# Two softmax attentions in steps of four heads, and a routed layer that gathers its tokens by indirect transfers

## The chip, the cores and the metric

The kernel runs on one core of a Trainium2 chip as one program. The metric is the time of one execution on the device in microseconds. Two runs of the kernel before took 3570.28 and 3580.17 us (median 3575.23). The engines are TensorE (PE, with its weight loads as PEld), VectorE (DVE), ScalarE (ACT), GpSimd (POOL) and SyncE (SP), which only issues transfers. ACT and POOL can issue transfers too, from their own queues.

## The reference

Four layers follow one another on x of shape (32, 256, 128): each adds an attention-like block of the normalised x, and then a feed-forward block of the normalised x. Three of these eight blocks matter here.

- The feed-forward block of layer 0. A softmax over 16 experts gives every token 16 scores. In each batch row (256 tokens) every expert takes the 32 tokens that score highest for it, computes `(gelu(x Wg) * (x Wu)) Wd` with 256 hidden channels, weighs the result with the score and adds it back at the token's place. A shared expert of the same form runs over all tokens.
- The attention of layer 2: 16 heads of 8 channels over 256 tokens, causal, with q, k and v through a rank-32 bottleneck: `softmax(q k^T / sqrt(8)) v`, then an output matrix.
- The attention in the feed-forward block of layer 3: again 16 heads of 8 channels over 256 tokens, with biases and without a mask. A routed expert layer follows it.

All of it is in float32; the attentions of the kernel split q and k into a high and a low half for it.

## The kernel before, in words

**Attention** (`attention`, lines 1118 to 1411) serves both softmax attentions. Heads are taken in pairs: one on partitions 0 to 63 (j = 0), the other on partitions 64 to 127 (j = 1). A batch has 8 pairs, and there are 32 batches. Its pieces are:

- `project` (transpose of x), `split` (q for i = 0, k for i = 1; high and low half, through DRAM into the layout by heads) and `load_values`. `split` writes each half twice into a DRAM tile `d` (line 1218), and reads it back with one transfer of 32 partitions for each j (line 1224). For q it also clears two rows (line 1226, `q<-k`).
- `maxima`: scores with queries on the partitions into a tile `s` of two PSUM banks, one for each head, and a single DVE reduction over both (line 1259).
- `lower` and `place`: the negated maxima, split into halves and turned into rows. DVE copies the rows out of PSUM (line 1287), and four transfers on SP put them into the q tile (line 1292, `q<-row`), so that the next scores come out with the maximum already subtracted.
- `weights`: scores with keys on the partitions into two tiles `t`, and two ACT exponentials (line 1314).
- `values`: exponentials times values, four heads together, into `o` (line 1327).
- `collect`, `turn`, `back` and `finish`: division by the sum, output matrix, addition.

For the causal attention, `cover` (line 1182) adds a large negative number to hidden scores by bf16 matmuls, all of one head and then all of the other.

PSUM has 8 banks: two buffers of `s` (pool `ps`, 4 banks), one bank for `o` (`pa`), and a ring of three (`pt`) that `weights` shares with `project`, `split`, `load_values`, `place`, `turn`, `back` and `finish`.

The order on PE, ACT and DVE is the program's (`manual_schedule`). In step t, one pair: `maxima` of the pair 14 steps ahead (`LEAD`), `weights` of pair t, the pieces that are due in that step (table `todo`), and, on every odd step, `values` of the two pairs before. SP and POOL are ordered by the planner of the framework. The q, k and v tiles are rings of four batches (`RING`).

**Layer 0 experts** (`l0_ffn`, lines 425 to 660) have four phases, ordered by the planner: (1) normalise, transpose, router logits, softmax; (2) `choose` (the 32 best of each of 8 rows x 16 experts, four times) and `shared` (16 blocks of 512 tokens); (3) gather: for each batch row a matmul spreads the chosen indices (line 590), DVE compares them with the token numbers (line 597), and two matmuls pick the tokens (line 600); (4) the 16 experts, two halves of 16 batch rows each (lines 624 to 631), and then the scatter by one-hot matmuls for each batch row (lines 643 to 659).

Of the kernel before, what the change touches and what calls it, by code (L numbers as in the profile page):

```python
# [18 lines left out]
P = 128  # L19
# [405 lines left out]
def l0_ffn(K):  # L425
    nc, ins = K.nc, K.ins
    NE, CAP, F = 16, 32, 256
    ES = NE * CAP
    with ExitStack() as es:
        sp = K.pool(es, "f0", 1)  # L430
        xn = sp.tile([P, NT, D], F32, name="xn")


        idx = sp.tile([P, 4, CAP], F32, name="idx")
        tab = sp.tile([P, 4, 2, 8, 4], F32, name="tab")
        gate_w = K.load(sp, "f0_gate_w")
# [4 lines left out]

        same_e = sp.tile([P, NE], F32, name="same_e")
        nc.vector.tensor_reduce(
            same_e, K.ident.rearrange("p (b e) -> p e b", e=NE), axis=AX.X, op=ALU.add
        )
        sel_b = sp.tile([P, 8, P], F32, name="sel_b")
        nc.vector.tensor_copy(
            sel_b,  # L450
            K.block_rows(sp, "blk8", 8).unsqueeze(2).to_broadcast([P, 8, P]),
        )
# [7 lines left out]
        tok = sp.tile([P, 2], F32, name="tok")  # L460
        nc.gpsimd.iota(
            tok, pattern=[[P, 2]], base=0, channel_multiplier=1,
# [8 lines left out]
        with ExitStack() as ts:  # L471
            xp = K.pool(ts, "f0x", 1)
            wk = K.pool(ts, "f0w", 2)
            xnT = xp.tile([P, NBLK, 512], F32, name="xnT")
            sc = xp.tile([P, 2, NB, NE], F32, name="sc")
            with ExitStack() as ps:
                pt = K.pool(ps, "f0pt", 2, PSUM)
                pl = K.pool(ps, "f0pl", 1, PSUM)
                lg = pl.tile([P, 2, NB, NE], F32, name="lg")
                for blk in range(NBLK):  # L480
                    for j in range(4 * blk, 4 * blk + 4):
                        K.normed(xn[:, j, :], j, mean, r)
                    t = pt.tile([P, 512], F32, name="t")
                    K.transpose4(t, xn[:, 4 * blk : 4 * blk + 4, :])
                    nc.scalar.copy(xnT[:, blk, :], t)
                    for i in range(4):
                        nc.tensor.matmul(
                            lg[:, i % 2, 2 * blk + i // 2, :],
                            xnT[:, blk, i * P : (i + 1) * P], gate_w, start=True, stop=True,
                        )  # L490
                K.softmax(
                    xp, sc.rearrange("p h b e -> p (h b) e"), lg.rearrange("p h b e -> p (h b) e")
                )

            pt = K.pool(ts, "f0pt2", 1, PSUM)
            pg = K.pool(ts, "f0pg", 2, PSUM)
            po = K.pool(ts, "f0po", 2, PSUM)

            def choose(q):

                t = pt.tile([P, SEQ], F32, name="st")
                for h in range(2):
                    nc.tensor.transpose(
                        t[:, h * P : (h + 1) * P],
                        sc[:, h, 8 * q : 8 * q + 8, :].rearrange("p b e -> p (b e)"), K.ident,
                    )
                s = wk.tile([P, SEQ], F32, name="s")
                nc.vector.tensor_copy(s, t)
                vi = wk.tile([P, 2, CAP], F32, name="vi")
                iu = wk.tile([P, CAP], mybir.dt.uint32, name="iu")  # L510
                for k in range(CAP // 8):
                    m = vi[:, 1, 8 * k : 8 * k + 8]
                    nc.vector.max(m, s)
                    nc.vector.max_index(iu[:, 8 * k : 8 * k + 8], m, s)
                    if k < CAP // 8 - 1:
                        nxt = wk.tile([P, SEQ], F32, name="s")
                        nc.vector.match_replace(nxt, m, s, -1.0)
                        s = nxt
                nc.vector.tensor_copy(vi[:, 0, :], iu)
                nc.gpsimd.tensor_copy(idx[:, q, :], vi[:, 0, :])  # L520
                vt = pt.tile([64, P], F32, name="vt")
                nc.tensor.transpose(vt, vi.rearrange("p k s -> p (k s)"), K.ident)
                vs = wk.tile([64, P], F32, name="vs")
                nc.vector.tensor_copy(vs, vt)
                o = pt.tile([P, 2, P], F32, name="st")
                for k in range(2):
                    nc.tensor.matmul(
                        o[:, k, :], rep[:, k].rearrange("p a s -> p (a s)"), vs,
                        start=True, stop=True,
                    )  # L530
                own = wk.tile([P, 64, 4], F32, name="own")
                nc.vector.tensor_mul(
                    own, o.rearrange("p k (n a) -> p (k n) a", a=4),
                    own4.unsqueeze(1).to_broadcast([P, 64, 4]),
                )
                nc.vector.tensor_reduce(
                    tab[:, q].rearrange("p k b g -> p (k b g)"), own, axis=AX.X, op=ALU.add
                )

            def shared(blk):  # L540
                h = wk.tile([P, 2, 512], F32, name="h")
                for c in range(2):
                    g = pg.tile([P, 512], F32, name="g")
                    u = pg.tile([P, 512], F32, name="u")
                    cs = slice(c * P, (c + 1) * P)
                    nc.tensor.matmul(g, wsg[:, cs], xnT[:, blk, :], start=True, stop=True)
                    nc.tensor.matmul(u, wsu[:, cs], xnT[:, blk, :], start=True, stop=True)
                    nc.scalar.activation(h[:, c, :], g, AF.Gelu)
                    nc.vector.tensor_mul(h[:, c, :], h[:, c, :], u)
                o = po.tile([P, 4, D], F32, name="o")  # L550
                for i in range(4):
                    for c in range(2):
                        nc.tensor.matmul(
                            o[:, i, :], h[:, c, i * P : (i + 1) * P], wsd[:, c, :],
                            start=c == 0, stop=c == 1,
                        )
                xb = K.x[:, 4 * blk : 4 * blk + 4, :]
                nc.vector.tensor_add(xb, xb, o)

            for q in range(4):  # L560
                choose(q)
                for blk in range(4 * q, 4 * q + 4):
                    shared(blk)


        xs = K.pool(es, "f0s", 1).tile([P, 4, NB, 4, CAP], F32, name="xs")
# [8 lines left out]

        experts = [expert(0), expert(1)]
        with ExitStack() as ps:
            gw = K.pool(ps, "f0g", 2)
            pi = K.pool(ps, "f0pi", 2, PSUM)
            px = K.pool(ps, "f0px", 2, PSUM)  # L580
            for q in range(4):
                bd = gw.tile([P, NE, CAP], F32, name="bd")
                nc.gpsimd.tensor_mul(
                    bd, idx[:, q, :].unsqueeze(1).to_broadcast([P, NE, CAP]),
                    same_e.unsqueeze(2).to_broadcast([P, NE, CAP]),
                )
                for b8 in range(8):
                    b = 8 * q + b8
                    ib = pi.tile([P, ES], F32, name="ib")
                    nc.tensor.matmul(  # L590
                        ib, sel_b[:, b8, :], bd.rearrange("p e s -> p (e s)"),
                        start=True, stop=True,
                    )
                    xg = px.tile([P, ES], F32, name="xg")
                    for h in range(2):
                        pick = gw.tile([P, ES], F32, name=f"pick{h}")
                        nc.vector.tensor_scalar(
                            pick, ib, tok[:, h : h + 1], None, ALU.is_equal
                        )
                        nc.tensor.matmul(  # L600
                            xg, xn[:, 2 * b + h, :], pick, start=h == 0, stop=h == 1
                        )
                    nc.scalar.copy(
                        xs[:, :, b].rearrange("p g a s -> p g (a s)"),
                        xg.rearrange("p (g n) -> p g n", g=4),
                    )


        with ExitStack() as ps:
            hw = K.pool(ps, "f0h", 2)  # L610
            pg = K.pool(ps, "f0eg", 3, PSUM)
            po = K.pool(ps, "f0eo", 2, PSUM)
            for e in range(NE):
# [492 lines left out]
HEADS, HD = 16, 8  # L1106
PAIRS = HEADS // 2
ONE = HD
LEAD = 14
RING = 4  # L1110


# [903 lines left out]
```

## Time and profile before

The profiled execution took 3567.47 us, with a span of 3565.8 us from the first to the last instruction.

| stretch, us from the start | what runs | PE busy | DVE | ACT | POOL | granted clock |
|---|---|---|---|---|---|---|
| 468 to 558 | layer 0: choose and shared | 88.5 | 57.5 | 20.4 | 2.9 | 0.98 |
| 558 to 649 | layer 0: gather by matmul | 88.3 | 45.1 | 18.7 | 2.1 | 1.00 |
| 649 to 822 | layer 0: experts | 173.0 | 65.4 | 38.2 | 0.0 | 1.00 |
| 822 to 903 | layer 0: scatter | 75.3 | 52.6 | 17.2 | 41.9 | 1.00 |
| 1900 to 2200 | layer 2 attention, steady part | 276.5 | 170.8 | 153.2 | 30.6 | 0.98 |
| 2750 to 3050 | layer 3 attention, steady part | 259.2 | 212.5 | 190.2 | 16.7 | 0.99 |

Busy times are in us. A busy PE is not PE at its peak, since the ends of matmuls are modelled. The granted clock is the share of TensorE's full clock that the chip allowed, and it takes the values 0.5 and 1 in stretches of some 3.4 us. The layer 2 attention runs from about 1710 to 2340 us, the one in layer 3 from about 2550 to 3220 us: together more than a third of the span.

### The profile page before, as it was taken

What the parts mean: (1) busy time and instruction counts of PE and PEld (TensorE: products, weight loads), DVE (VectorE), ACT (ScalarE), POOL (GpSimd) and SP (SyncE); (2) the same over time, 40 slices, a digit from 0 to 9 for tenths busy, and PEclk for the clock granted to TensorE, in tenths of its full rate; (3) what the DMA queues carried; (4) which work ended last, traced back from release to release, by engine and by line L of the source; (5) the groups of instructions that cost most, each with busy time, mean ns of one, the idle gap of its engine ahead of it and who ended that gap; (6) DMA issues with size and microseconds to landing.
All of it is one profiled execution on the core that took longest, in us unless ns stands there. A gap on an engine that the chain in (4) does not pass through costs nothing.

```text
span 3565.8 us, 56988 instructions
## 1 busy us (share of the span) xinstructions
PE 2669.6 (75%) x20984; PEld 1837.9 (52%) x20984; DVE 1843.4 (52%) x4383; ACT 1321.5 (37%) x2729; POOL 843.5 (24%) x1023
## 2 busy tenths in 40 slices
PE   2499799999797825995399999976728888886054
PEld 1255564347466614995266666666415555555043
DVE  5353555435767111224755555545836677756167
ACT  2363222222532302442045555521205666663044
POOL 2302100003234554553311111000180000000645
PEclk9999789999896967997599999967859999995588
DMA  4073000010002114776244444301124444420264
GB/s 97 0 233 111 18 1 1 24 34 1 4 5 112 38 41 150 225 235 193 69 123 123 124 128 124 99 3 76 57 63 126 128 126 130 130 81 1 90 181 125
DMA packets 235473, 323.52 MB, mean 91 GB/s; under 512 B 37846, under 2 KB 203699, under 8 KB 225981
## 3 DMA queue, kind: packets, MB, share of 16 engines
q1 hardware_dynamic: 212044, 282.82, 26.8%
q0 software_dynamic: 14336, 30.57, 2.4%
q10 hardware_dynamic: 8816, 6.49, 0.6%
q8 instruction: 167, 2.74, 0.3%
q14 instruction: 110, 0.89, 0.1%
HBM read 197.19 MB, written 119.44 MB: 89 GB/s over the span
## 4 chain that ended last, share of the span: by engine, by line
PE 29%; DMA 12%; DVE 11%; issue 6%; ACT 5%; POOL 5%; SPq 2%; POOLq 0%; ACTq 0%; DVEq 0%
DMA k<-d 7%; ACT e L1314 4%; PE o L1327 3%; PE s L1251 3%; DMA bin<-xs,at 3%; PE hp L1045 3%; PE o L1063 3%; PE t L1306 3%; POOL y L1631 1%; POOL bin L1744 1%; DMA d<-half 1%; PE t L1345 1%; PE t L1236 1%; PE t L1205 1%; PE t L1368 1%
## 5 line engine op out<-in xcount | busy, mean ns | idle before, releaser
L1259 DVE TENSOR_REDUCE top<-s 128x6 f32<-128x768 f32 (+1 forms) x512 | 546.4, 1089 | 361.8 <-PE s L1182 217.7
L1314 ACT ACTIVATE e<-t 128x384 f32<-128x384 f32 (+1 forms) x1024 | 502.0, 543 | 412.5 <-PE t L1182 237.0
L1251 PE MATMUL s<-k,q 64*128 64x256 f32 (+1 forms) x2048 | 281.1, 334 | 68.3 <-DMA k<-d 58.1
L1306 PE MATMUL t<-q,k 64*128 64x256 f32 (+1 forms) x2048 | 282.9, 302 | 35.8 <-ACT e L1314 31.0
L1251 PEld LDWEIGHTS s<-k,q 64*128 64x128 f32 x2048 | 173.3, 194 | 192.2 <-issue 98.8
L1327 PE MATMUL o<-e,val 128*32 128x256 f32 (+1 forms) x4096 | 251.7, 364 | 0.0
L1306 PEld LDWEIGHTS t<-q,k 64*128 64x128 f32 x2048 | 194.8, 189 | 76.8 <-ACT e L1314 70.2
L1050 ACT ACTIVATE h<-hp,w 128x256 f32<-128x256 f32 x288 | 119.0, 470 | 269.7 <-issue 144.6
L1070 POOL DMA_INDIRECT res<-y,gx x144 | 137.8, 957 | 148.5 <-DVE y L1068 66.5
L1327 PEld LDWEIGHTS o<-e,val 128*32 128x32 f32 x4096 | 108.6, 110 | 96.5 <-issue 40.8
L972 POOL DMA_INDIRECT bin<-xs,at x128 | 123.1, 962 | 98.3 <-DVE at L966 39.1
L1440 POOL TENSOR_SCALAR xn<-x_sb,mean_a,r_a 128x128 f32<-128x128 f32 x64 | 50.1, 792 | 392.0 <-PE t L1195 391.7
L1063 PEld LDWEIGHTS o<-w,h 128*128 128x128 f32 x1152 | 139.8, 192 | 3.7
L1068 DVE TENSOR_TENSOR y<-o,b 128x256 f32<-128x256 f32 x72 | 30.6, 425 | 213.9 <-PE o L1063 207.0
L1063 PE MATMUL o<-w,h 128*128 128x128 f32 x1152 | 140.1, 275 | 0.0
L1045 PE MATMUL hp<-xT,w 128*128 128x256 f32 x576 | 138.9, 385 | 0.0
L966 DVE COPY at<-at 128x1 uint32<-128x1 uint32 x128 | 19.7, 154 | 187.8 <-DMA bin<-xs,at 187.6
L1654 POOL TENSOR_TENSOR y<-y,b_f_bo 128x256 f32<-128x256 f32 x32 | 23.5, 735 | 386.8 <-PE t L1195 386.7
L1032 PE MATMUL t<-ident,gx 128*128 128x128 f32 x144 | 28.4, 280 | 111.8 <-DMA gx<-bin 111.8
L1045 PEld LDWEIGHTS hp<-xT,w 128*128 128x128 f32 x576 | 105.6, 193 | 12.0 <-issue 0.2
L114 PE MATMUL t<-ident,xn 128*128 128x128 f32 x256 | 59.7, 369 | 58.7 <-DVE xn L107 58.7
L646 POOL TENSOR_SCALAR put<-pos,tab 128x256 f32<-128x256 f32 x32 | 40.5, 1267 | 256.0 <-PE o L630 219.6
(487 smaller groups left out, 5803.5 us busy)
## 6 DMA issues: line engine op xcount, KB each, us to landing
d<-half SPq DMA_DIRECT2D x256, 256.0 KB
w<-in_f_w SPq DMA_DIRECT2D x72, 514.0 KB
tz<-kpad SPq DMA_DIRECT2D x64, 512.0 KB
q<-d SPq DMA_DIRECT2D x128, 256.0 KB
k<-d SPq DMA_DIRECT2D x128, 256.0 KB
bin<-blank SPq DMA_DIRECT2D x4, 2580.0 KB
gx<-bin SPq DMA_DIRECT2D x40, 258.0 KB
w<-in_f_w SPq DMA_DIRECT2D x40, 257.0 KB
```

The source lines that it names most:

```text
L114: self.nc.tensor.transpose(ps[:, i * P : (i + 1) * P], xn[:, i, :], self.ident)
L972: sends.append(link(K, "f1send", nc.gpsimd.indirect_dma_start(out=bin_, out_offset=bass.IndirectOffsetOnAxis(ap=at, axis=0), in_=xs[:, j, ...
L1045: nc.tensor.matmul(hp[:, i, :], w[:, c * P : (c + 1) * P], xT, start=i == 0, stop=i == 1)
L1050: nc.scalar.activation(h[:, c, :], hp[:, i, :], AF.Gelu, bias=w[:, FC * P + c : FC * P + c + 1],)
L1063: nc.tensor.matmul(o[:, s, :], h[:, c, s * P : (s + 1) * P], w2[:, c, :], start=s == 0 and c == 0, stop=s == 1 and c == FC - 1,)
L1070: backs.append(link(K, "f1back", nc.gpsimd.indirect_dma_start(out=res, out_offset=bass.IndirectOffsetOnAxis(ap=x[:, s, D : D + 1].bitcast( ...
L1251: nc.tensor.matmul(s[:, j, lo:hi], q[r, p, h * P : (h + 1) * P], k[r, p, 0 : hi - lo], start=h == 0, stop=not causal and h == 1,)
L1259: nc.vector.tensor_reduce(live["top", b][:, :, :, p].rearrange("q h j -> q j h"), s[:, :, 0:used].rearrange("q j (h k) -> q j h k", h=n), ...
L1306: nc.tensor.matmul(ts[j][:, kh * SEQ : kh * SEQ + SEQ - late], k[r, p, kh * P : (kh + 1) * P], q[r, p, late:SEQ], start=kh == 0, stop=not ...
L1314: nc.scalar.activation(e[:, j, :], ts[j], AF.Exp)
L1327: nc.tensor.matmul(o[32 * i : 32 * i + 32, g, late:SEQ], val[b % RING][:, kh, at : at + 32], es[i // 2][:, i % 2, kh * SEQ : kh * SEQ + SE ...
L1440: nc.gpsimd.tensor_scalar(xn[:, i, :], K.x[:, j, :], mean[:, j : j + 1], r[:, j : j + 1], ALU.subtract, ALU.mult,)
```

## The change

In the attention a step is now two pairs (four heads): `weights` 0, `maxima` 0, `values` of the step before, then pieces that are due, `weights` 1, `maxima` 1, and pieces that are due. `maxima` runs 7 such steps ahead. Each head's scores for the maxima have a bank of their own, from a pool of three single banks, with one DVE reduction for each head. The pieces that shared the ring with `weights` get one bank of their own (`pm`). `cover` alternates between the two heads. Each half of q and k is written to DRAM once, and read back with eight transfers of 8 partitions for each of q and k. In `place` the row copy and the four `q<-row` transfers move from DVE and SP to ACT.

```diff
-    ps = K.pool(es, tag + "ps", 2, PSUM)
+    ps = K.pool(es, tag + "ps", 3, PSUM)
     pt = K.pool(es, tag + "pt", 3, PSUM)
     pa = K.pool(es, tag + "pa", 1, PSUM)
+    pm = K.pool(es, tag + "pm", 1, PSUM)
...
-        d = dp.tile([2, 2, P, SEQ], F32, name=f"d{i}")
+        d = dp.tile([2, P, SEQ], F32, name=f"d{i}")
         for n in range(2):
-            nc.sync.dma_start(
-                (d[n] if i == 0 else d[:, n]).rearrange("r p s -> p r s"),
-                half[n].bitcast(F32).unsqueeze(1).to_broadcast([P, 2, SEQ]),
-            )
-        d = d.rearrange("m n (c j p) s -> j (m n c) p s", j=2, p=PAIRS)
-        for j in range(2):
-            nc.sync.dma_start(to[64 * j : 64 * j + 4 * HD].bitcast(F32), d[j])
-            if i == 0:
+            nc.sync.dma_start(d[n], half[n].bitcast(F32))
+        d = d.rearrange("m (c j p) s -> m j c p s", j=2, p=PAIRS)
+        for n in range(4):
+            m = (n // 2, n % 2)[i]
+            for j in range(2):
+                at = 64 * j + n * HD
+                nc.sync.dma_start(to[at : at + HD].bitcast(F32), d[m, j])
+        if i == 0:
+            for j in range(2):
                 nc.sync.dma_start(
...
-        nc.vector.tensor_copy(row, t.rearrange("n h q -> n (h q)"))
+        nc.scalar.copy(row, t.rearrange("n h q -> n (h q)"))
...
-                nc.sync.dma_start(
+                nc.scalar.dma_start(
                     qrys[b % RING][at : at + 1].bitcast(F32),
...
+    quads = PAIRS // 2
     for b in range(NB):
...
+        first, there = quads * b - AHEAD, quads * b
+        at(first - 7, 1, fetch, b)
+        at(first - 6, 1, project, b)
+        at(first - 5, 0, split, b, 0)
+        at(first - 5, 1, split, b, 1)
+        at(first - 4, 1, load_values, b)
+        at(first + quads - 1, 2, lower, b)
+        at(first + quads, 0, place, b)
+        last = there + quads - 1 + behind
+        at(last, 3, collect, b)
+        at(there + 6, 0, turn, b)
+        at(there + 6, 1, back, b)
+        at(there + 7, 0, finish, b)
...
+        for step in range(-AHEAD - 7, NB * quads + 5):
+            quad(weights, step, 0)
+            quad(maxima, step + AHEAD, 0)
+            quad(values, step - behind, None)
+            run(step, 3)
+            run(step, 0)
+            quad(weights, step, 1)
+            quad(maxima, step + AHEAD, 1)
+            run(step, 2)
+            run(step, 1)
```

In layer 0 the normalised tokens are stored to a DRAM tile `rows`. `choose` also gives row numbers (`place`), and POOL gathers the chosen tokens with 128 indirect transfers of 128 rows, four for each batch row, each after a small index copy on POOL into one of two `at` tiles. `turn` transposes what came. The experts run over the first 16 batch rows and then over the second 16, each expert's weights being loaded twice. Gathers stand beside the shared blocks and the first half, scatters of the first half beside the second half. This part is still ordered by the planner.

```diff
+        def gather(b):
+            x = gp.tile([P, 4, D], F32, name="gx")
+            for g in range(4):
+                at = ap.tile([P, 1], U32, name="at")
+                nc.gpsimd.tensor_copy(at, place[:, b // 8, b % 8, g : g + 1])
+                nc.gpsimd.indirect_dma_start(
+                    out=x[:, g, :], out_offset=None, in_=rows,
+                    in_offset=bass.IndirectOffsetOnAxis(ap=at, axis=0),
+                )
...
+        for blk in range(1, NBLK):
+            gather(blk + 1)
+            shared(blk)
+            turn(blk - 1)
...
+        order = [(e, hb) for hb in range(2) for e in range(NE)]
...
+            if n + 17 < NB and n < NE:
+                gather(n + 17)
+            routed(e, hb, experts[n])
+            if hb == 0:
+                turn(16 + n)
+            elif e:
+                scatter(e - 1)
+        for b in range(15, NB):
+            scatter(b)
```

## Prediction

> **What bounds the kernel now.** I read the table of busy times first, then the chain of waits, and then stretches of single attention batches. No engine is full over the span:
>
> ```profile
> PE 2669.6 (75%) x20984; PEld 1837.9 (52%) x20984; DVE 1843.4 (52%) x4383; ACT 1321.5 (37%) x2729; POOL 843.5 (24%) x1023
> ...
> L1314 ACT ACTIVATE e<-t 128x384 f32<-128x384 f32 (+1 forms) x1024 | 502.0, 543 | 412.5 <-PE t L1182 237.0
> ```
>
> The chain of waits in order of time shows what closes a batch of an attention (layer 3 here):
>
> ```profile
> 2895.97 1.00 PE o L1327 x16
> 2896.97 0.43 PE s L1251 x4
> 2897.40 0.28 PE t L1306 x4
> ...
> 2897.73 0.60 ACT e L1314
> 2898.34 0.04 issue
> 2898.38 0.51 PE t L1306 x3
> 2898.89 0.52 SPq L1226
> ...
> 2899.91 3.91 DMA k<-d
> 2903.82 0.04 issue
> 2903.86 0.50 PE s L1251 x3
> ```
>
> PE runs values, scores, weights; then the second tile of the next `weights` waits for the first exponential to free a bank, and once a batch PE waits for k. k<-d pieces recur every 17.1 us in layer 2 (2015.04, 2032.17) and 16.95 in layer 3 (2882.96, 2899.91). So a batch is a loop of PE and ACT with short waits, and what delays an exponential delays PE. Stage windows say the same of layer 0: in the gather (558 to 649 us) PE is busy 88.3 of 91 us, in the experts 173.0 of 173; it is PE's.
>
> **Attention, the steps without `place`.** A step of two pairs without extra pieces is two intervals. From weights 0 to weights 1 PE is never short of work: weights 0.36 us in layer 2 (0.3 in layer 3), maxima 0.5 (0.3), values 0.79 (1.0), together some 1.8 in layer 2 and 1.65 in layer 3 with the starts after the wait. From weights 1 to weights 0 of the next step the bank decides: 0.70 us (0.49) from the first matmul to the exponential, 0.49 (0.60) for it, 0.05 to PE: 1.24 (1.14). That is 3.05 and 2.8 us. Before, two pairs took 3.07 (2014.07 to 2017.14, values to values) and 2.91 (2895.90 to 2898.81), since the loop is the same. The new order wins elsewhere: pieces behind maxima 1 (project 0.37, second split 0.55, load_values 0.64, back 0.37) lie in the wait for the bank, 0.4 us long in layer 2 and 0.6 in layer 3, and no longer take banks from that ring. Pieces before weights 1 stay on the path: split 0.55, place 0.22, turn 0.5, finish 0.65 = 1.9. Left over: 0.4 to 0.65 where the second split waits for DVE to empty the one bank `pm`, 0.3 for back, 0.3 for load_values: 1.0 (1.25). A batch is then 4 x 3.05 + 1.9 + 1.0 = 15.1 us in layer 2, and 4 x 2.8 + 1.9 + 1.25 = 14.35 in layer 3. Alternating the heads in `cover` (bf16 pieces of 0.09 to 0.15 us a pair) I put at -0.3 a batch, between 0 and all 1.9 us of them; nearest 0, as they are already short.
>
> The split reductions cost DVE little: 0.955 us for 768 elements and 1.222 for 1024 give 1.04 ns an element, so two halves cost 0.1 us more a pair; DVE is busy 57% and 71% of the steady parts, which hides it. Three single banks for `s` ask the first reduction of a pair to end about 1.5 us after weights 1; PE comes to need it then, too, so I take 0 (to 0.1 us a step, 25 us in all, without that cover).
>
> **Attention, the step with `place`.** The row copy (ACT, as the 128x256 copies: 0.38 us) and four transfers come before the exponentials of weights 1 in ACT's program. The issue of a `q<-row` on SP, and one transfer that both queues issue in turn:
>
> ```profile
> L1292 SPq DMA_DIRECT2D q<-row x256: 623/634/963, 1777.5 to 3200.5; - x128
> ...
> L1094 ACTq DMA_DIRECT2D y<-res x8: 366/366/532, 1658.5 to 1689.1; - x8
> L1094 SPq DMA_DIRECT2D y<-res x8: 359/359/382, 1658.7 to 1691.2; - x8
> ```
>
> The queues charge alike, so ACT pays 0.63 us each; four in a row took 2.75 us on SP. Queued behind them are two exponentials, and for these waits PE. In layer 3 the exponentials start 3.4 us after place's transposes (0.2 + 0.2 to the copy, 0.38, 2.75), and free the bank at 4.0; PE has weights 1, maxima 1 and load_values, 1.3 us. It stands still for **2.7 us**; in layer 2, with 1.55 us of work, for 2.4. A batch becomes 17.05 us in layer 3 (now 16.95) and 15.1 - 0.3 + 2.4 = 17.2 in layer 2 (now 17.1): 32 x 0.1 + 32 x 0.1 = **+6 us**. The gain of the order is spent on ACT's queue. Bounds for the hold: 0 (the issue overlaps the exponentials), -163 us; 0.96 us each (L1292's longest), +85.
>
> **The clock.** A standstill of 2.4 to 2.7 us is new; the waits on PE in the steady parts are now at most 1.6. Windows of 3.41 us, cut where the granted clock may change; columns are PE, PEld, DVE, ACT, POOL busy, clock, DMA share, GB/s:
>
> ```profile
> 2157.74:2161.15 3.41, 2.01 (x20) 1.41 (x20) 1.01 (x2) 0.65 (x2) 0.94 (x2) 1.00 0.07 14
> 2161.15:2164.56 3.41, 3.41 (x23) 2.80 (x24) 2.18 (x7) 1.85 (x5) 0.23 (x1) 0.50 0.44 149
> 3140.78:3144.19 3.41, 1.85 (x18) 1.01 (x10) 0.60 (x1) 0.73 (x3) 0.22 (x1) 1.00 0.05 10
> 3144.19:3147.60 3.41, 2.70 (x16) 2.03 (x15) 2.55 (x6) 2.60 (x6) 0.23 (x1) 0.50 0.29 96
> ```
>
> Two windows with PE busy under 60% are each followed by one at half clock. Over all such windows at full clock, PE busy under half was followed by half clock 14 times in 15, 50 to 80% 8 times in 103, over 80% never in 442. A gap of 2.4 to 2.7 us leaves more than half of some window idle in 7 to 8 of 10 positions. Now about 1 batch in 10 has a drop; I take 65% of 64 batches more: 42. Price: such a batch took 18.30 us (2155.48 to 2173.78, +1.2) and 19.77 (2796.26 to 2816.03, +2.8); mean 2.0. So **+84 us** (0 to 64 x 2.8 = 179). [...]
>
> **The halves and their transfers.** Stores halve. Loads go from 2 to 8 for a split: SP issues 16 x 0.37 = 5.9 us a batch instead of 1.5, less the 2.5 us of q<-row. The last k now lands 4.9 us after the last scores of a batch (2898.89 to 2903.82 above); with eight issues it is about 0.5 + 8 x 0.37 + 3.9 = 7.4 from the same point, if the planner leaves the order. The new schedule has some 10 pairs from split to maxima where 8 were. I take 0, bounds -0.7 (today's wait gone) and +2.5 us a batch. [...] No run here has such loads; the nearest row is q<-k, 16 KB into two partitions, with 3.54 us in the chain against 3.5 to 4.4 for the 256 KB of k<-d.
>
> **Layer 0.** POOL's sends in layer 1 are the nearest row:
>
> ```profile
> 1162.06 0.19 POOL L968 COPY xs<-home 128x4 uint32<-128x4 uint32 x1 [1.47 <-DMA bin<-xs,at]
> 1162.79 0.97 POOL L972 DMA_INDIRECT bin<-xs,at  x1 [0.54 <-DVE x_sb L996]
> 1164.06 0.96 POOL L972 DMA_INDIRECT bin<-xs,at  x1 [0.30 <-issue]
> ```
>
> A gather is copy 0.19, 0.54, transfer 0.96 and 0.2 to 0.3 to the next: 1.9 us; between 1.27 (no copy) and 3.16 (1159.63 to 1162.79, one in flight). From 488 us, when the first choice is done, 64 gathers end at 610 and the sixteenth row is turned at 613; PE (16 x (5.1 + 0.66)) would be done at 570 and waits. The second 64 end at 735, PE's first half (16 x (5.4 + 0.66) = 97) is hidden beneath. The second half is PE's: 16 x 5.4 + 15 x 2.4 = 122, and 17 scatters at 2.5 = 43: end at 900 instead of 903. **-4 us**, from -70 (1.27, where PE is the bound) to +160.
>
> **Sum** against the profiled execution, 3567.5: +6 + 84 - 4 = 3653.5. The median of the runs is 7.8 higher: **3661 us**.
>
> **Rivals.**
> - *The clock holds.* Against it are the windows above; for it, that drops lasted one or two windows. 3575 + 6 - 4 = 3577.
> - *ACT does not hold the exponentials* (the other side): the issues pass beside them, batches fall to 14.35 and 14.8, 32 x 2.6 + 32 x 2.3 = -157, six drops of 2.0 go too: 3575 - 157 - 12 - 4 = 3402. Against it: the transfers stand before the exponentials in one queue. It is 2% faster as soon as the four hold ACT for less than some 1.6 us together.
> - *k comes late*: +2.5 x 64 = 160 on the forecast, 3821. For it, the chain through SP above; against, the longer lead.
> - *Gathers go one at a time*, so the self-pacing does not happen: 3661 + 164 = 3825.
>
> **Chances.** Forecast 0.44 (own range 3620 to 3710), clock holds 0.20, ACT free 0.18, k late 0.14, gathers singly 0.04. Faster, same and slower are split at 2%, about what a measurement of this kernel tells from no change: 3504 and 3647. All of ACT free is faster, 0.18; the second case and a fifth of the forecast are the same, 0.28; the rest is slower, 0.54. The range leaves out most of ACT free: from 3500, under the second case with the gathers at their best (3511), to 3840.
>
> **What will show it.** Right: in the steady attention one PE wait of 2.4 to 2.7 us a batch, ended by the exponential, just after ACT's four issues; granted clock well under 0.98 there; periods of 18 to 19 us; layer 0 ending near 900. Wrong: issues on ACT near 0.1 us, a clock still at 0.98, PE waiting for k<-d over 1 us a batch, or gathers spaced far from 1.9 us.

## The result, and the profile after

The changed kernel takes **4062.43 us** (median of 4052.25 and 4072.61) against 3575.23: 1.136 times the time before, 95% interval 1.122 to 1.150. The forecast was 3661, at most 3840. The sign was right and the size was not: +487 us, where +86 was forecast.

The profiled execution took 4052.25 us with a span of 4050.3. First the table of busy times and the costliest group of ACT, then PE's and SP's waits (what was waited for: us in total, times, longest):

```profile
PE 2839.3 (70%) x20920; PEld 1920.7 (47%) x20920; DVE 1832.3 (45%) x4768; ACT 1353.2 (33%) x2793; POOL 990.1 (24%) x1271
...
L1310 ACT ACTIVATE e<-t 128x384 f32<-128x384 f32 (+1 forms) x1024 | 502.6, 544 | 470.3 <-PE t L1179 176.4
```

```profile
PE s L1250 <- DMA k<-d: 273.5, 62, 8.5
...
PE t L1303 <- ACT e L1310: 83.3, 72, 3.2
```

```profile
SPq L1221 <- DMA q<-row: 269.1, 61, 39.2
...
SPq L1224 <- PE s L1179: 170.7, 26, 8.1
```

Before, the wait for k was a fifth of that (the scores of `maxima`, and what ended PE's idle time before them):

```profile
L1251 PE MATMUL s<-k,q 64*128 64x256 f32 (+1 forms) x2048 | 281.1, 334 | 68.3 <-DMA k<-d 58.1
```

PE executes nearly as many matmuls as before and is 170 us longer busy with them: it runs slower. (With the changed kernel's own matmuls and an undisturbed attention, e3 below, it is busy 2559.6 us.) It waits once a batch for k, and once for the exponential behind `place`. The chain of waits in layer 2 has both, one after the other (start, us, what; line 1284 is the row copy, 1289 `q<-row`, 1221 the loads of split, 1224 `q<-k`):

```profile
2004.86 0.37 ACT row L1284
2005.23 0.02 issue
2005.25 0.63 ACTq L1289
...
2005.97 0.94 ACTq L1289
2006.91 0.04 issue
2006.95 0.63 ACTq L1289
2007.58 0.04 issue
2007.61 0.63 ACTq L1289
2008.24 0.05 issue
2008.29 0.50 ACT e L1310
...
2015.83 0.19 PE s L1179 x4
2016.02 0.01 SPq L1224
...
2017.91 0.30 SPq L1221
2018.21 0.04 issue
2018.25 5.80 DMA k<-d
2024.05 0.04 issue
2024.10 0.42 PE s L1250
```

The upper half is the forecast's standstill: four issues of 0.63 to 0.94 us and the exponential behind them. In this kernel PE stands still there for only 0.9 us a batch in layer 2 and 1.4 in layer 3. The lower half is what the forecast took as 0: SP sends `q<-k` after a wait that PE ends, and the eight loads of k behind it; the last of them lands 5.80 us after its issue, and PE's next scores wait for it. Over 1850 to 2250 us the chain has 11 such pieces, 4.8 us on average (3.28 to 6.04); before, it had 23 in the same stretch, 3.95 us on average (3.71 to 4.40).

Stretches of 300 and 400 us in the steady attentions of layers 2 and 3 (PE, PEld, DVE, ACT, POOL busy, granted clock, DMA share, GB/s):

```profile
1850.00:2150.00 300.00, 251.27 (x2688) 166.43 (x2687) 134.22 (x303) 120.28 (x289) 23.54 (x39) 0.79 0.31 71
2900.00:3300.00 400.00, 261.32 (x2097) 154.92 (x2096) 175.28 (x322) 156.74 (x322) 13.58 (x28) 0.74 0.26 58
```

Where the 484.5 us between the two spans lie, by the times of the 64 row copies of `place`: the 31 periods of layer 2 grew from 539.8 to 720.7 us (+180.9), those of layer 3 from 529.6 to 841.3 (+311.7). The first row copy of layer 2 comes 25.5 earlier, between the attentions are 14.6 more, behind them 2.9. All of the loss is in the two attentions.

### The profile page after: what moved, and what is told of

It reads as the page before. It is cut to its first block, busy times and chain, and to the rows that moved or that the text cites. A ratio compares the mean times of both kernels' runs of the same rounds, so it can differ in the third digit from the quotient of the medians.

```text
span 4050.3 us, 58374 instructions
## 1 busy us (share of the span) xinstructions
PE 2839.3 (70%) x20920; PEld 1920.7 (47%) x20920; DVE 1832.3 (45%) x4768; ACT 1353.2 (33%) x2793; POOL 990.1 (24%) x1271
## 4 chain that ended last, share of the span: by engine, by line
PE 46%; DMA 14%; DVE 13%; issue 8%; POOL 7%; ACT 5%; ACTq 4%; SPq 3%; DVEq 0%; POOLq 0%
PE o L1323 7%; DMA k<-d 6%; ACTq L1289 4%; PE t L1303 4%; PE s L1250 4%; DMA bin<-xs,at 3%; PE hp L1039 3%; PE o L1057 3%; SPq L1221 2%; DMA gx<-rows,at 2%; POOL gx L554 2%; PE o L622 1%; PE m L1341 1%; PE m L1202 1%; PE p L313 1%
## 5 line engine op out<-in xcount | busy, mean ns | idle before, releaser
L1257 DVE TENSOR_REDUCE top<-s 128x3 f32<-128x384 f32 (+1 forms) x1024 | 588.2, 619 | 754.4 <-PE s L1250 422.9
L1250 PE MATMUL s<-k,q 64*128 64x256 f32 (+1 forms) x2048 | 328.0, 364 | 325.8 <-DMA k<-d 273.5
L1250 PEld LDWEIGHTS s<-k,q 64*128 64x128 f32 x2048 | 233.1, 234 | 359.3 <-issue 228.8
L1303 PE MATMUL t<-q,k 64*128 64x256 f32 (+1 forms) x2048 | 314.6, 359 | 83.5 <-ACT e L1310 83.3
L1323 PE MATMUL o<-e,val 128*32 128x256 f32 (+1 forms) x4096 | 325.1, 446 | 0.3 <-ACT e L1310 0.2
L1284 ACT CAST row<-m 32x256 fp32r<-32x256 f32 x64 | 23.2, 362 | 485.9 <-PE m L1280 485.9
L1323 PEld LDWEIGHTS o<-e,val 128*32 128x32 f32 x4096 | 125.5, 128 | 121.9 <-issue 82.6
L554 POOL DMA_INDIRECT gx<-rows,at x128 | 124.9, 976 | 42.5 <-POOL at L553 33.1
L1179 PE MATMUL s<-hideq,eye 64*128 64x256 bf16 (+1 forms) x1024 | 116.4, 291 | 0.0
L579 DVE TENSOR_TENSOR h<-h,g 128x512 f32<-128x512 f32 x96 | 65.7, 684 | 94.4 <-PE g L577 81.3
```

The source lines that it names most:

```text
L554: nc.gpsimd.indirect_dma_start(out=x[:, g, :], out_offset=None, in_=rows, in_offset=bass.IndirectOffsetOnAxis(ap=at, axis=0),)
L1250: nc.tensor.matmul(ss[j][:, lo:hi], q[r, p, h * P : (h + 1) * P], k[r, p, 0 : hi - lo], start=h == 0, stop=not causal and h == 1,)
L1257: nc.vector.tensor_reduce(live["top", b][:, :, j, p], ss[j][:, 0:used].rearrange("q (h k) -> q h k", h=n), axis=AX.X, op=ALU.max, negate=True,
L1303: nc.tensor.matmul(ts[j][:, kh * SEQ : kh * SEQ + SEQ - late], k[r, p, kh * P : (kh + 1) * P], q[r, p, late:SEQ], start=kh == 0, stop=not ...
L1323: nc.tensor.matmul(o[32 * i : 32 * i + 32, g, late:SEQ], val[b % RING][:, kh, at : at + 32], es[i // 2][:, i % 2, kh * SEQ : kh * SEQ + SE ...
```

## The experiments

The kernels of one table row are compared by this: the period is from one row copy of `place` to the next, averaged over the 20 batches from the ninth on; idle is the time in them in which no matmul ran, for each batch; both are from the trace's records of single instructions. The first number of a pair is layer 2, the second layer 3. Times of before are 3561, 3566, 3560 and 3562 us in the four groups of runs (e1 to e4, e5 to e8, e10 to e12, e13). e2, e4, e5, e6, e8 and e10 were run once, the changed kernel twice, the others four times.

| kernel | us | period | PE idle a batch | clock |
|---|---|---|---|---|
| before | 3575 | 17.50, 17.12 | 1.36, 2.39 | 0.99, 0.98 |
| changed | 4062 | 23.91, 28.53 | 4.18, 9.87 | 0.81, 0.76 |
| e1: loads of 32 partitions | 3703 | 19.36, 21.40 | 2.00, 4.70 | 0.89, 0.85 |
| e2: place on DVE and SP | 3866 | 23.54, 22.44 | 5.91, 6.19 | 0.84, 0.83 |
| e3: both | 3395 | 15.22, 15.16 | 0.04, 1.16 | 1.00, 1.00 |
| e4: e1, eight loads by columns | 3796 | 23.03, 20.65 | 5.15, 4.15 | 0.83, 0.85 |
| e8: e3, eight loads by columns | 3735 | 20.52, 21.32 | 3.22, 4.69 | 0.90, 0.83 |
| e5: before, new loads alone | 4019 | 23.85, 25.63 | 4.66, 5.79 | 0.81, 0.70 |
| e6: before, new place alone | 3642 | 18.68, 18.28 | 2.37, 3.76 | 0.95, 0.97 |
| e7: before, new layer 0 alone | 3526 | 17.55, 17.07 | 1.44, 2.42 | 1.00, 0.99 |
| e10: e1, two of four on SP | 3442 | 16.02, 15.93 | 0.49, 1.57 | 1.00, 0.99 |
| e11: e1, idle PE kept busy | 3636 | 18.14, 19.77 | 0.10, 0.84 | 1.00, 1.00 |
| e12: e3, row copy on ACT | 3385 | 15.20, 14.82 | 0.03, 0.89 | 1.00, 1.00 |
| e13: e12, k stored once | 3430 | 15.36, 16.25 | 0.09, 1.90 | 1.00, 0.97 |

**Undoing one part, and both.** Theory L says that late loads are the main cause, theory P that ACT's queue is. e1 gives `split` its transfers back:

```diff
-        d = dp.tile([2, P, SEQ], F32, name=f"d{i}")
+        d = dp.tile([2, 2, P, SEQ], F32, name=f"d{i}")
...
+        for j in range(2):
+            nc.sync.dma_start(to[64 * j : 64 * j + 4 * HD].bitcast(F32), d[j])
```

> The changed kernel with the transfers of split as before: each half stored twice, and read back by two transfers of 32 partitions for q and two for k. The row copy and the four q<-row transfers stay on ACT. Theory L (late loads are the main cause): eight loads of 8 partitions take 7.1 us from first to last packet in the changed kernel, two of 32 partitions took 2.0 us before; with them gone the waits for k<-d fall from 273 us to under 70, batches fall from 23.3 and 27.1 us to 18 to 19, and the time is 3600 to 3660, which is the forecast's own sum with layer 0 at -25 instead of -4. Theory P (ACT's queue is the main cause): the batches stay above 21 us and the time above 3850, since nothing of ACT is touched.

Measured 3702.6 us, 1.037 of before (1.032 to 1.042): 43 us above what theory L expected, and far below theory P's 3850. 352 of the 487 us go (1.136 less 1.037, of 3561), so the loads are the larger part. PE's largest wait is now the exponential, and it is the forecast's standstill; the rows are PE's waits, and then ACT and PE at one `place` of layer 3:

```profile
PE t L1302 <- ACT e L1309: 191.3, 73, 5.7
```

```profile
3008.22 4.72 ACTq L1288 DMA_DIRECT2D q<-row  x4
...
3012.99 1.09 ACT L1309 ACTIVATE e<-t 128x512 f32<-128x512 f32 x2 [4.80 <-DMA q<-row]
...
3013.64 0.79 PE L1302 MATMUL t<-q,k 64*128 64x256 f32 x3 [4.22 <-ACT e L1309]
```

In layer 2 the four issues took 2.96 us and PE stood still 2.05; here they took 4.72, as there are waits between them, and PE stood still 4.22.

e2 moves the row copy to DVE and `q<-row` to SP, and leaves the new loads; e3 does both.

```diff
-        nc.scalar.copy(row, t.rearrange("n h q -> n (h q)"))
+        nc.vector.tensor_copy(row, t.rearrange("n h q -> n (h q)"))
...
-                nc.scalar.dma_start(
+                nc.sync.dma_start(
```

> The changed kernel with place as before: the row copy on DVE, the four q<-row transfers on SP. The loads of 8 partitions stay. Theory L: the loads still come late, now behind four more issues on SP; PE's wait at place, 2.0 to 3.2 us a batch, goes, but PE then only waits the longer for k; 3950 to 4070. Theory P: batches fall by the 2.4 to 2.7 us that the forecast gave the standstill and by its clock drops, 64 x (2.5 + 1.3) = 243 us or more; under 3820.

Measured 3865.9 us, between the two: place is worth some 197 us even here (one run), but what PE waits for was not foreseen. It is no longer k, but `q<-row`, which now stands behind the loads in SP's queue. PE's wait, and SP's order in one batch:

```profile
PE t L1303 <- DMA q<-row: 352.2, 59, 9.6
```

```profile
2024.00 2.54 SPq L1215 DMA_DIRECT2D d<-half  x3
2026.63 2.96 SPq L1221 DMA_DIRECT2D q<-d  x8
2029.70 0.35 SPq L1215 DMA_DIRECT2D d<-half  x1
2030.37 7.56 SPq L1221 DMA_DIRECT2D k<-d  x8
2038.03 2.79 SPq L1289 DMA_DIRECT2D q<-row  x4
```

> The changed kernel with both parts as before: transfers of split in 32 partitions, halves stored twice, place on DVE and SP. What is left is the order in steps of four heads, the banks, cover by turns, and layer 0. If the order is worth what the forecast worked out (15.1 and 14.35 us a batch against 17.1 and 16.95) and layer 0 gives 25 us: 3575 - 32 x 2.0 - 32 x 2.6 - 25 = 3403. If the order gains nothing, since k is late by the same chain through SP as before: 3550.

Measured 3395.05 us, 0.954 of before (0.952 to 0.956), 8 us from the expected 3403. Part of that closeness is luck: layer 3 is 0.8 us a batch longer than the sum had it, and layer 0 gives 40 us (e7) instead of 25. In layer 2 PE has nothing left to wait for, and the clock stays full (same columns as the stretches above):

```profile
1850.00:2150.00 300.00, 299.12 (x4226) 205.96 (x4224) 215.43 (x494) 181.36 (x433) 34.47 (x58) 1.00 0.51 146
2650.00:2950.00 300.00, 276.38 (x2962) 171.90 (x2962) 250.69 (x476) 219.26 (x436) 19.27 (x40) 1.00 0.51 144
```

So with e3 as the ground, place on ACT costs 307 us (e1), the new loads 471 (e2), both 667: each of the two alone more than eats the order's gain, which is 131 us (e7 less e3).

**Eight issues, or 8 partitions?** e4 and e8 have the changed kernel's number of load issues, but each load goes to 32 partitions and two of the eight pairs, in pieces of 2 KB instead of 8 (halves stored twice).

```diff
+            for g in range(4):
+                nc.sync.dma_start(
+                    to[64 * j : 64 * j + 4 * HD, 2 * g : 2 * g + 2].bitcast(F32),
+                    d[j][:, 2 * g : 2 * g + 2],
+                )
```

> The kernel of e1 with as many load issues as the changed kernel, eight for q and eight for k, but each to 32 partitions and two of the eight pairs (2 KB pieces) instead of 8 partitions and all pairs. Stores are doubled as in e1. If the number of issues on SP, and the waits of each for a transfer eight issues earlier, make k late: within 100 us of the changed kernel's 4062. If it is the few partitions that a transfer goes to: at most 40 us above e1.

> The kernel of e3 (order of four heads, place on DVE and SP, halves stored twice), but with eight loads a split, each to 32 partitions and two of the eight pairs. Against e2, which has the same number of issues on the same queues with 8 partitions each and took 3866. If the number of issues and their waits are what costs 471 us: 3750 to 3870. If it is the few partitions of a transfer: 3395 to 3470.

Both fell between: e4 took 3796 (93 above e1, and 266 below the changed kernel), e8 3735 (340 above e3, 131 below e2). Two costs are there, and it depends on the place of `q<-row` which one is large. With it on SP (e8) the count of issues decides: the loads keep SP's queue some 9 us a batch, `q<-row` goes out behind them, and PE waits for it:

```profile
PE t L1306 <- DMA q<-row: 183.8, 88, 4.7
```

SP of e8, and the same stretch in e12, which has two loads for q and two for k:

```profile
2007.54 4.11 SPq L1222 DMA_DIRECT2D q<-d  x8
2011.70 4.92 SPq L1222 DMA_DIRECT2D k<-d  x8
2016.71 2.78 SPq L1292 DMA_DIRECT2D q<-row  x4
```

```profile
2016.96 0.87 SPq L1221 DMA_DIRECT2D q<-d  x2
2018.68 0.77 SPq L1221 DMA_DIRECT2D k<-d  x2
2019.50 2.69 SPq L1288 DMA_DIRECT2D q<-row  x4
```

With `q<-row` on ACT (changed, e1, e4) the count costs 93 and the 8 partitions, with the other size of the pieces, 266. The trace's records of single transferred pieces show the rate in layer 2 (20 batches). The 128 pieces of 8 KB of a batch's q and k (1 MB) take 4.5 to 6.1 us from first to last in e3, 172 to 232 GB/s. In the changed kernel the 66 pieces of a batch's k and one `q<-k` take 5.7 to 7.2 us, 75 to 94 GB/s (15 batches); there eight pieces run at a time, 0.8 to 0.9 us each while the queue is full, where one alone took 0.31. e4 and e8 move the 1 MB in 7.8 to 9.7 us, about the time of their sixteen issues.

The count also holds ACT. The built program lists for every transfer of SP and of ACT the counters that it waits for; a few of SP's rows, the transfer's own counter first:

```
1035 L1215 DMACopy d1_16033<-half11_16030 128x256 [waits DMAHW3_49,DVE_49]
1036 L1224 DMACopy q3_12107<-k3_12106 2x2048 [waits DMAHW4_49,PE_49]
1037 L1221 DMACopy k2_12095<-d1_16033 8x2048 [waits DMAHW5_49,DMAHW2_49]
1038 L1221 DMACopy k2_12095<-d1_16033 8x2048 [waits DMAHW6_49]
1039 L1221 DMACopy k2_12095<-d1_16033 8x2048 [waits DMAHW7_49,DMAHW3_49]
1040 L1221 DMACopy k2_12095<-d1_16033 8x2048 [waits DMAHW0_49]
```

Eight counters (DMAHW0 to 7) go round over the transfers of both queues: in the changed kernel's trace the 2271 transfers of SP and ACT are counted on eight, 283 or 284 on each. A transfer of this program waits until the one eight before it has landed, whatever it carries; a second entry is the transfer or the engine whose work it needs. That is why SP's loads waited 269 us for `q<-row` in the changed kernel, and why ACT's exponentials in e4 waited for a load of k that they do not use:

```profile
ACT e L1313 <- DMA k<-d: 170.7, 28, 7.0
```

**One part alone, on the kernel before.** The edits are those of the change: `split`'s transfers (e5), `place`'s five lines (e6), the function `l0_ffn` (e7).

> The kernel before with one part of the change alone: each half stored once, and q and k read back by eight transfers of 8 partitions each. If these transfers are slow by themselves (7.1 us for the eight of k against 2.0 for two), k, which PE already awaits once a batch by 0.4 to 1 us, is late by 5 us or more: 3561 + 64 x 5 = 3880 and above, with DMA k<-d at the head of PE's waits. If they only harm together with the new order: within 60 us of 3561.

Measured 4018.5 us, +452: the new loads do nearly all of the change's harm without any of its order. Of 17 last loads of k in layer 2 that the chain holds, the mean is 5.36 us (before 3.95), and PE waits for k:

```profile
PE s L1252 <- DMA k<-d: 190.2, 51, 26.2
```

> The kernel before with one part of the change alone: the row copy and the four q<-row transfers on ACT. The forecast's mechanism (four issues of 0.63 us hold the exponentials behind them) holds here too: 3.1 us of ACT's queue a batch, of which PE covers about 1.0 to 1.3, so 64 x 1.8 to 2.1 = 115 to 135 us, and the clock on top: 3680 to 3800. If the hold matters only in the new order: within 60 us of 3561.

Measured 3642.3 us, +76, below the expected 3680 to 3800. The standstill is there (one of 1.8 us a batch in layer 2, 2.2 in layer 3), but it takes the place of the shorter waits that the old order had: idle grows by 1.0 and 1.4 us a batch. And the clock falls in 13 and 11 of 29 batches, not in all.

> The kernel before with the new layer 0 experts alone. By the first profile after the change layer 0 ends at 875 instead of 903 us: 3561 - 25 to 30 = 3531 to 3536. By the forecast, which had -4: 3557.

Measured 3525.8 us, 0.988 of before (0.987 to 0.990): -40, somewhat more than expected. The last matmul of layer 0's scatter starts at 870.6 us, where the scatter before ran until 903, and the first row copy of layer 2 comes 30.5 us earlier. Behind the attentions the program is 5.6 us shorter, which is not explained. The gathers (all gather transfers: count, ns, first and last start) come every 1.63 us:

```profile
L554 POOL DMA_INDIRECT gx<-rows,at x128: 947/972/1242, 494.4 to 701.6; - x128
```

**The standstill by its size, and the clock.** e10 leaves two of the four `q<-row` on ACT, e11 leaves all four and fills the standstill with matmuls on a tile of zeros (`idle`).

```diff
-                nc.scalar.dma_start(
+                (nc.scalar, nc.sync)[j].dma_start(
```

```diff
+    def spin(b):
+        t = pm.tile([P, SEQ], F32, name="m")
+        n = 6 if causal else 11
+        for i in range(n):
+            nc.tensor.matmul(t, K.ident, idle, start=i == 0, stop=i == n - 1)
...
         at(first + quads, 0, place, b)
+        at(first + quads, 2, spin, b)
```

> The kernel of e1 (3703 us: transfers of split in 32 partitions, place on ACT), with the two q<-row transfers of the upper heads moved to SP; the row copy and the other two stay on ACT. If PE's standstill is the time of ACT's issues, it shrinks by two of them, 1.4 us: in layer 2 from 2.0 to 0.6 us a batch, too short for a drop of the clock, in layer 3 from 4.1 to about 2.7: 3395 + 32 x 0.6 + 32 x 3 = 3510, between 3450 and 3560. If it is not the issues but q<-row arriving late, nothing is won: 3650 and above.

Measured 3441.9 us, 8 below the expected range. With two issues fewer on ACT, and without the waits between the four, 261 us are won from e1. By the table 32 x (1.51 + 3.13) = 148 of them are idle time of PE. The rest goes with the clock, which hardly falls any more (in 29 batches of each layer it fell in none of layer 2 and one of layer 3; e1 had 25 and 29).

> The kernel of e1 with matmuls added whose result nobody reads, just after the scores of place's step, where PE then stands still: 6 a batch (2.1 us) in layer 2, 11 (3.9 us) in layer 3, 0.35 us each. If the half clock that follows a standstill is a cost of its own, it goes: the granted clock in the steady parts returns from 0.89 and 0.85 to 0.97 or more, batches fall from 19.4 and 21.4 us to 17.2 and 18.2, and the time to 3540 to 3580 although PE does more work. If the standstill alone costs, the time stays at 3703 or rises.

Measured 3636.2 us, 1.021 of before (1.018 to 1.024), 66 less than e1 although PE now does 2.9 and 5.0 us of useless work a batch. Each of the added matmuls became two instructions of 0.24 us, so the filling was longer than the standstill and set the batch; the expected 3540 to 3580 was missed, most likely for that. The stretches of e1 and then of e11 show the clock:

```profile
1850.00:2150.00 300.00, 269.09 (x3289) 181.66 (x3288) 163.12 (x371) 148.21 (x357) 28.82 (x48) 0.88 0.39 111
2800.00:3200.00 400.00, 312.72 (x2813) 190.71 (x2813) 233.06 (x431) 210.77 (x433) 18.15 (x37) 0.85 0.36 101
```

```profile
1850.00:2150.00 300.00, 298.38 (x3724) 209.47 (x3724) 174.73 (x397) 158.79 (x379) 29.07 (x49) 1.00 0.44 124
2800.00:3200.00 400.00, 383.28 (x3467) 260.80 (x3466) 249.82 (x463) 227.50 (x461) 19.35 (x40) 1.00 0.40 113
```

With PE busy for 298.4 of 300 us and for 383.3 of 400 the clock stayed at 1.00, where e1 had 0.88 and 0.85, and that saved more than the overlong filling cost. In e1 PE is busy 2.2 us a batch longer than in e3 in layer 2 (19.36 less 2.00 idle, against 15.18) and 2.7 in layer 3 (16.70 against 14.00). Against e10, whose clock is full too, it is 1.8 and 2.3. So the half clock costs nearly as much as the standstill beside it in layer 2, and over half of it in layer 3.

**Better versions.** e12 takes e3 and leaves the row copy on ACT.

> The kernel of e3 (3395 us) with the row copy on ACT, while the four transfers stay on SP: the other half of what place moved. By the forecast's mechanism only the transfers hold ACT; the copy is 0.36 us, held ahead of the exponentials, beneath PE's 1.3 us of work in that stretch: 3395, within 15. In layer 3 DVE is busy 84% and PE waits 0.3 us a batch for its row copy, so it may be up to 10 us faster. If the copy were the cause of e1's loss: 3500 and above.

Measured 3385.1 us, 0.951 of before (0.948 to 0.953), the fastest of all: layer 3 gains 0.34 us a batch. The copy was not the harm in e1; the transfers were. e13 stores the halves of k once, with loads of 16 partitions:

```diff
+        if i == 1:
+            d = dp.tile([2, P, SEQ], F32, name=f"d{i}")
...
+            d = d.rearrange("m (c j p) s -> j (m c) p s", j=2, p=PAIRS)
+            for j in range(2):
+                for n in range(2):
+                    at = 64 * j + 2 * n * HD
+                    nc.sync.dma_start(to[at : at + 2 * HD].bitcast(F32), d[j])
```

> The kernel of e12 (3385 us) with the halves of k stored once, and read back by four transfers of 16 partitions (128 KB) instead of two of 32 (256 KB); q stays stored twice. A step between 32 partitions and the changed kernel's 8. SP has two more issues a batch, about 1.1 us, ahead of q<-row. If the lead is long enough nothing waits: 3385, within 10. If transfers to 16 partitions are slow as those to 8, q<-row and k come later by 2 us or more a batch: 3450 and above.

Measured 3430.2 us, 0.963 (0.960 to 0.966), 45 above e12: neither value. The loads of k keep SP 1.75 us instead of 0.8 in layer 3, ahead of three of the four `q<-row`, and the 1 MB of q and k runs at 151 to 182 GB/s in layer 2 (18 of 20 batches) instead of 179 to 234 (19 of 20). Layer 2 hardly feels it; in layer 3 PE waits for `q<-row`, which it hardly did in e12. PE's waits in the two attentions of e13, and in layer 3 of e12:

```profile
PE t L1312 <- DMA q<-row: 28.9, 24, 1.9
```

```profile
PE t L1302 <- DMA q<-row: 0.5, 2, 0.3
```

The single pieces of k say why its loads are slower. Those that start 1.0 to 1.7 us after the last issue of k (layer 2, medians) run 16 at a time in e12 as in e13, but take 0.54 us each when the load goes to 32 partitions and 0.91 when it goes to 16: 241 against 143 GB/s. In the changed kernel, with 8 partitions, 8 run at a time and take 0.79 us: 83 GB/s. The loads of k in e13 and in the changed kernel also read each stored half twice; no run parts that from the number of partitions.

## Why the prediction was right or wrong

- **The order of four heads: right.** 14.8 (15.1 less 0.3 for `cover`) and 14.35 us a batch were forecast without `place`; e3 measured 15.22 and 15.16. As a gain the forecast had 2.3 and 2.6 us a batch, and e7 less e3 is 2.33 and 1.91. The 2.33 is luck in part: batches of the kernel before average 17.50 and 17.12 us, where the forecast had read 17.1 and 16.95 from a single one. In layer 3 the waits for DVE's copies out of the single bank are there (some 1.0 of 1.16 us of idle time a batch), but the forecast had 1.25 for them; the 0.8 more lies in PE's busy time, and no run shows in which piece.
- **`place` on ACT: right in mechanism, a fifth too small.** 0.63 us an issue and one standstill a batch ended by the exponential are in the traces as forecast. In e1, where nothing else is late, the standstill is 2.0 us in layer 2 (forecast 2.4) and 4.1 in layer 3 (2.7), as there are waits between the issues there (4.72 us for the four above, against 2.96 in layer 2). The hold was forecast at 163 us and its clock at 84, together 247; e1 less e3 is 307. That ACT's issues pass beside the exponentials, the rival on the other side, is refuted. In the changed kernel itself the standstill is only 0.9 and 1.4 us; its granted clock is 0.81 and 0.76, so that the work ahead of the wait takes longer, but that this is the reason was not tested.
- **The clock: real, and over half again the size.** 42 drops of 2.0 us were forecast, 84 us. In e1 it fell in 54 of 58 batches, and cost 1.8 to 2.2 and 2.3 to 2.7 us a batch: 133 to 156 us. The rival that it holds fell with e1 and e11. In layer 2 of e1, one gap of 2.0 us a batch brought 25 drops in 29 batches.
- **The halves and their transfers: this is the step that failed.** The forecast took 0, and as its upper bound 2.5 us a batch, 160 us. Measured are 352 us (changed against e1), 471 (e2 against e3) and 452 (e5): 5.5 to 7.4 us a batch.

  The lateness itself was worked out nearly right: k was to land 7.4 us after the last scores of a batch, and in the chain above it lands 8.0 us after them (2016.02 to 2024.05). Wrong was to set the longer lead (10 pairs instead of 8) against it and take the sum as 0. In layer 2 the loads of k stand on SP behind a `q<-k` for the next batch (row 1036 of the list above), which waits until PE has done with that tile (PE_49): in all 17 batches from 1850 to 2250 us SP waited there, 6.5 us each, and the loads started only then. In layer 3 the loads waited for counters of earlier `k<-d`, `q<-row` and `q<-d` (87.6, 82.5 and 25.0 us in 21 batches from 2900 to 3500), 9.3 us a batch. The issues were priced rightly: the eight of k go out in some 2.9 us, 0.36 each; it is in e4 and e8 that they cost 0.5.

  The rate was wrong too. The row that stood for loads to few partitions, `q<-k`, has two pieces of 8 KB and says nothing of 64 in a queue: the eight loads of k ran at some 83 GB/s, where the two before ran at 156 to 240 (layer 2). And PE's new waits took the clock with them: by the table, of 374 us between e1 and the changed kernel (periods), 235 are idle time and 139 slower matmuls. The rival "k comes late" had the right mechanism and a third to a half of the price.

  In layer 2, pieces of a batch's sixteen loads (and of its two `q<-k`) were under way for 12.1 to 13.5 us (16 batches of the changed kernel).
- **Layer 0: right in sign, too small.** -4 was forecast; e7 gives -40, of which 30 lie in layer 0: the gathers come every 1.65 us in the changed kernel instead of 1.9, its experts start at 598 instead of 613, and the second half and the scatter take 155 us (717 to 872) instead of 165.

The parts alone sum to +452 + 76 - 40 - 131 (the order, e3 against e7) = +357, less than the 487 measured: place costs 76 us in an order that has idle time to give, and 307 in one that has none. With the 197 that it costs beside the late loads (changed against e2) the sum is +478. What stays open is why the loads of 8 partitions are slow. In e13 those of 16 were slower a piece though as many pieces ran at once, so the number that run at once is not all of it; how much each part costs, no run shows.

## What to carry to other kernels

A transfer's price is its place in a queue: count the issues that stand ahead of it, on every queue that shares its completion counters, and what each of them waits for, before the bytes. A longer lead in the program's order was worth nothing here while the loads of k stood behind a transfer that waited (6.5 us a batch in layer 2). Halving the stored bytes by cutting the loads from 32 partitions to 8 lost 350 to 470 us: the same megabyte came in four times as many issues at under half the rate. A PE that had just been made full (0.04 us idle a batch in layer 2 of e3) had no idle time left to hide a new wait of 2 us, and paid for it twice: in e1 2.0 us a batch in standing, and 1.8 to 2.2 in the clock.

## What the runs showed of the hardware

- **In these traces the clock fell behind windows with PE busy under half, with or without a long gap.** The granted clock changed on a grid of 3.41 us (all 46 stretches of one clock in the trace of before begin on it, and all 186 of the changed kernel's). Over the fourteen traces here, a window of this grid at full clock with PE busy under half was followed by half clock 498 times in 510; with 50 to 60% 101 in 184; 60 to 70% 39 in 729; over 70% 5 in 8313. Windows under half that touched no gap over 1.7 us were followed by half clock 53 times in 54; windows of 60 to 70% that touched one of over 3.4 us, 14 times in 52. In layer 2, e10's gap of 0.4 us a batch brought no drop in 29 batches, and e1's of 2.0 brought 25.
- **Half clock lasted while PE was busy under 80% of its windows.** A window at half clock with PE busy under 80% was never followed by full clock (0 in 2720; over 80%, 629 in 1746). In e1's layer 2 a stretch of half clock lasted 5.6 us on average with PE 99% busy in it, in the changed kernel's layer 3 10.1 with PE 63% busy.
- **Loads of 16 partitions were slower a piece than loads of 32.** Pieces of 8 KB took 0.54 us with 16 at a time in e12's loads of k (32 partitions) and 0.91 with 16 at a time in e13's (16).
- **Transfers of two engines were tied together** by the eight counters that this program gives them: in e4 late loads of SP held ACT's next `q<-row`, and with it the exponentials (170.7 us, 28 times).
